# A four-layer graph network on one core: the first tile's table rows fetched in two steps, and the places of the buffers laid out anew

## The chip, the cores and the metric

The kernel runs on one core of a Trainium2 chip. The time is the device time of one execution in microseconds (us), lower is better. The core has five engines with a queue of instructions each: PE (TensorE, matrix products), DVE (VectorE), ACT (ScalarE), POOL (GpSimd) and SP (SyncE, which here only issues transfers). Sixteen DMA engines carry the transfers. POOL issues the gathers, transfers whose rows are picked by a list of indices; SP issues the plain ones.

## The reference

Four graph layers on 2708 nodes with 128 features. Each normalizes x, applies relu to get h, and adds its result to x. `adj` is a 2708 x 2708 matrix. The change lies in the second layer (layer 1):

```python
XW = X @ W
s_col = XW @ a[0, :f]
s_row = XW @ a[0, f:]
Z1 = leaky_relu(s_row[:, None] + s_col[None, :], 0.01)
den = exp(Z1)
num = A @ den
att = where(num != 0, den / where(num != 0, num, 1.0), 0.0)
H = A @ (att @ XW)
```

Layers 0, 2 and 3 are also built on products with `adj`. Layer 2 and layer 3 are one such product each, followed by a 128 x 128 product.

## The kernel before

**Tiles.** A tile is 128 nodes: T = 22 tiles, the last (tile 21) has 20. A stretch of 2708 columns is worked in six blocks of 512 (the last 148), one PSUM bank (`acc0` to `acc5`) each.

**The idea of layer 1.** For a fixed column j, `den[k, j]` depends on k only through whether `s_row[k] + s_col[j]` is positive. So `num[:, j]` needs no product with `den`: if the nodes k are sorted by falling `s_row`, it is a combination of two neighbouring rows of a table of running sums. The kernel ranks the nodes, and `fetch` (L1589) gathers the rows of `adjT` in rank order, 125 per tile, to tiles called `mov`. `make_knots(t)` (L1702) multiplies them by a triangular weight, which gives 128 table rows ("knots", three places of a tile repeat its neighbour's), copies them out of PSUM on DVE and ACT by turns, puts the last two rows into the next `mov` tile, and SP writes them to a table in device memory (L1735). Tile t of the table is rows 128t to 128t + 127; the last one has 96 rows. The last two tiles' writes and the first's are cut in two halves. Each row has 2708 floats, 10.8 KB.

**Which rows a node needs.** ACT counts for every column node how many row scores are above the negative of its own (`signs_of`, L1564 on). `row_places` (L1678 on) turns the count q into the number of the first of the two rows, `pair_u`. Places grow with q. It runs for tiles 0 to 7 behind `make_knots(5)`, for 8 to 15 behind `make_knots(12)`, and for the rest behind `make_knots(18)`. `knots_around` gathers two floats per node and is issued on POOL, at most three per turn of the loop.

**The loop around the seam** (L1740 on) does, for each t: fetch tile t + 3, up to three `knots_around`, `make_knots(t)`, then signs, places, weights. Every instruction that matters is recorded in program order on its engine (`pin`, `Ordered`, L84), so the lines of the code are the order of the queues.

**The last pass of layer 1** (L1775 on) takes the tiles in the order 21, 0, 1, ..., 20 (`ORDER`). `gather(t)` (L1786) fetches the two rows of every node of tile t in one packet per node, 21.7 KB, into a pair buffer of 128 x 2 x 2708 floats; there are three. `divided` (DVE) combines the two rows into an attention tile, `inverted` (ACT) takes a logarithm and an exponential, `limited` (DVE) finishes, `weighed` (PE) multiplies with XW. Attention tiles and, later, the chunks of `adj` come from a pool of five (`big`). Three gathers are issued ahead, the next always behind the `divided` that frees its pair buffer. All gathers read `table[:, :]`, so they wait until the last table row is written.

**The places.** Up to the seam `big` has four buffers. Behind the last table the pools of layer 1 (`l1`), of the rows (`rows`, from which the table is written) and `big` are closed, `big` is opened again with five buffers, and the pair buffers are laid over the rest.

**Behind the pass** the chunks of `adj` for the product A @ (att @ XW) are loaded by SP: three while the pass ends (L1863), then in `aggregate` (L392). Of its 22 chunks the last six (16 to 21) are "resident": they are loaded once into a pool `t_res` (L1879) and stay for layers 2 and 3. Chunks 16 to 18 are asked for behind the fourth chunk.

Of the kernel before, what the change touches and what calls it, by code (L numbers as in the profile page):

```python
# [17 lines left out]
P = 128  # L18
# [6 lines left out]
def kernel(  # L25
# [18 lines left out]
    nc = tc.nc  # L44
    N, D = x.shape
    assert D == P
    T = -(-N // P)
# [5 lines left out]
    TAIL_RES = 6  # L53
# [10 lines left out]

    lay = ctx.enter_context(tc.tile_pool(name="lay", bufs=1))

    big_open = ExitStack()
    big = big_open.enter_context(tc.tile_pool(name="big", bufs=4))
    dram = ctx.enter_context(tc.tile_pool(name="dram", bufs=1, space=DRAM))
    ps_s = ctx.enter_context(tc.tile_pool(name="ps_s", bufs=2, space=PSUM))  # L70
    ps_a = ctx.enter_context(tc.tile_pool(name="ps_a", bufs=1, space=PSUM))
# [14 lines left out]
    pe, dve, act = Ordered(nc.tensor), Ordered(nc.vector), Ordered(nc.scalar)  # L86

    resident = {}
    pools = {}
# [4 lines left out]
    def chunk(i):  # L94
        if i in resident:
            return resident[i]
        if i >= T - pools["n"]:
            c = resident[i] = pools["res"].tile([P, N + 1], F32, name=f"res{i}")
        else:
            c = big.tile([P, N + 1], F32, name="chunk", tag="big")  # L100
        t = tile_at(i)
        pin(nc.sync.dma_start(c[: width(t), :N], adjT[t * P : t * P + width(t), :]))
        if i == T - 1:
            pools["apart"] = True
        return c
# [133 lines left out]
    with nc.allow_non_contiguous_dma(reason="256 elements"):  # L239
# [16 lines left out]
        out=above, in_=ones_b, pattern=[[1, P]], compare_op=ALU.is_ge, fill=0.0, base=-1, channel_multiplier=-1  # L256
# [17 lines left out]
    for v, first, fill in ((1, 3, float(P // 2)), (2, 2, -1e5)):  # L274
        nc.gpsimd.affine_select(
            out=empty[:, v, :], in_=empty[:, v, :], pattern=[[0, T]],
# [3 lines left out]
            out=empty[:, v, :], in_=empty[:, v, :], pattern=[[-PER, T]],  # L280
# [389 lines left out]
    c = len(COLS) - 2  # L670
# [127 lines left out]
    for t in range(T):  # L798
        w = width(t)
# [170 lines left out]
    def vec(name, n=T, dt=F32):  # L970
        return keep.tile([P, n], dt, name=name)
# [718 lines left out]

    def knots_around(t):
        w = width(t)
        pin(
            nc.gpsimd.indirect_dma_start(
                out=around[:w, t, :],
                out_offset=None,
                in_=knot_at[:, :],
                in_offset=bass.IndirectOffsetOnAxis(ap=knot_u[:w, t : t + 1], axis=0),
            )
        )  # L1700

    def make_knots(t):  # L1702
        m = moving.pop(t)
        o = rowtile("knots")
        p = [acc(b) for b in range(NKB)]
        for b, (k0, n) in enumerate(KBS):
            pe.matmul(p[b][:, :n], wt[:, t, :], m[:, k0 : k0 + n], start=True, stop=(t > 0))
        if t == 0:
            pieces = []
            for b, (k0, n) in enumerate(KBS):  # L1710
                inside = []
                for g in range(4):
# [16 lines left out]
        for b, (k0, n) in enumerate(KBS):  # L1729
            (dve.tensor_copy if b % 2 else act.copy)(o[:, k0 : k0 + n], p[b][:, :n])  # L1730
            if t < T - 1:
                dve.tensor_copy(moving[t + 1][:2, k0 : k0 + n], o[:2, k0 : k0 + n])
        n = P if t < T - 1 else LAST
        for c in (slice(0, HALF), slice(HALF, N)) if t in (0, T - 2, T - 1) else (slice(0, N),):
            pin(nc.sync.dma_start(table[t * P : t * P + n, c], o[:n, c]))  # L1735

    BATCHES = {5: (0, 8), 12: (8, 16), 18: (16, T)}
    unsigned = list(range(1, T))
    near = []
    for t in range(T):  # L1740
        if t + 3 < T:
            fetch(t + 3)
        for _ in range(min(len(near), 3)):
            knots_around(near.pop(0))
        make_knots(t)
        for _ in range(2 if t in (3, 7) else 1):
            if unsigned:
                signs_of(unsigned.pop(0))
        if t in BATCHES:
            row_places(*BATCHES[t])  # L1750
            near.extend(range(*BATCHES[t]))
        if t % 4 == 0 and t // 4 + 1 < NG:
            weights(t // 4 + 1)
        if t % 3 == 2 and t // 3 < NG:
            weighted(t // 3)
# [16 lines left out]
    act.activation(row_all, row_all, AF.Exp, bias=forty)  # L1772


    l1.close()  # L1775
    rows_open.close()
    big_open.close()
    big = ctx.enter_context(tc.tile_pool(name="big", bufs=5))
    between = ExitStack()
    pairs = between.enter_context(tc.tile_pool(name="pairs", bufs=3, side="right"))  # L1780
    pools.clear()
    pools.update(n=TAIL_RES)
    py = [acc(b) for b in range(NKB)]
    rows, attention = {}, {}

    def gather(t):  # L1786
        w = width(t)
        r = rows[t] = pairs.tile([P, 2, N], F32, name="pair", tag="pair")
        pin(
            nc.gpsimd.indirect_dma_start(  # L1790
                out=r[:w].rearrange("p a n -> p (a n)"),
                out_offset=None,
                in_=table[:, :],
                in_offset=bass.IndirectOffsetOnAxis(ap=pair_u[:w, t : t + 1], axis=0),
            )
        )
# [8 lines left out]
    def divided(t, some=slice(0, 3)):  # L1805
        w = width(t)
        r = rows[t]
        if t not in attention:
            attention[t] = big.tile([P, N + 1], F32, name="att", tag="big")
        at = attention[t]  # L1810
        for c in cuts(t)[some]:
            dve.scalar_tensor_tensor(
                at[:w, c], r[:w, 0, c], kap[:w, t : t + 1], r[:w, 1, c], op0=ALU.mult, op1=ALU.add
            )
# [29 lines left out]
                stop=(t == ORDER[-1]),  # L1844
            )

    for t in ORDER[:3]:
        gather(t)
    for x_, t in enumerate(ORDER[:-1]):
        divided(t)  # L1850
        if x_ + 3 < T:
            gather(ORDER[x_ + 3])
        inverted(t)
        if x_:
            limited(ORDER[x_ - 1])
            weighed(ORDER[x_ - 1])
    t, u = ORDER[-2:]
    first, rest_ = slice(0, 1), slice(1, 3)
    for i in range(3):
        c = big.tile([P, N + 1], F32, name="chunk", tag="big")  # L1860
        if i == 0:
            dve.memset(c[:1, :1], 0.0)
        pin(nc.sync.dma_start(c[:, :N], adjT[i * P : (i + 1) * P, :]))  # L1863
        resident[i] = c
        if i == 0:
            limited(t, first)
            divided(u, first)
            inverted(u, first)
            limited(t, rest_)
            weighed(t)  # L1870
            divided(u, rest_)
            inverted(u, rest_)
# [3 lines left out]


    tl = ctx.enter_context(ExitStack())
    pools.update(res=tl.enter_context(tc.tile_pool(name="t_res", bufs=1)))  # L1879
    yT = lay.tile([P, N], F32, name="yT", tag="U")  # L1880
    attended = lay.tile([P, T, D], F32, name="attended", tag="Y")
    for b, (k0, n) in enumerate(KBS):
# [135 lines left out]
```

## Time and profile before

| What | us |
|---|---|
| Median of 3 runs (1101.18 to 1101.49) | 1101.22 |
| The profiled execution, its time | 1102.7 |
| Its span in the profile | 1101.0 |
| Last table write issued | 616.2 |
| First pair gather issued on POOL | 621.6 |
| Pair gathers: number, POOL busy | 22, 66.6 |
| DVE waits for pair gathers, total | 21.5 |
| End of the pass on PE (the first product behind it starts) | 778.4 |

The profile shows one execution. Starts are counted from the start of the span. A line of the timeline gives the start, the duration, the engine, the line of the code, the operation, what is written from what, and in brackets how long the engine had been idle and what released it. A line of the stretch view gives the busy time of every engine between two moments, the share of full clock that PE was granted, the mean busy share of the 16 DMA engines, and what they moved in GB/s. Lines of helpers (L84) stand for many operations: there the names of the tiles tell them apart.

### The profile page before, as it was taken

The page shows a single profiled execution, that of the slowest core. Times are in us where ns is not written, and L with a number is a line of the kernel's source. Part 1 is how long each engine was busy: PE and PEld are TensorE (multiplying, and loading weights), DVE is VectorE, ACT ScalarE, POOL GpSimd, SP SyncE. Part 2 cuts the span into 40 slices and gives each one's busy share as a digit, 9 for nine tenths or more (in the row PEclk, how much of TensorE's full clock was granted, in tenths as well). Part 3 has the DMA queues.
Part 4 walks back from the last instruction along what each step waited for, and adds up shares of the span by engine and source line. Part 5 has one row for each costly group of instructions (what it writes and reads, how often), then busy time and mean ns, then how long its engine had stood idle before and what let it go on. Part 6 is the DMA issues. An engine that isn't in the chain of part 4 may idle for free.

```text
span 1101.0 us, 10182 instructions
## 1 busy us (share of the span) xinstructions
PE 998.3 (91%) x3553; PEld 487.2 (44%) x3553; DVE 584.2 (53%) x1203; ACT 403.0 (37%) x637; POOL 230.9 (21%) x248
## 2 busy tenths in 40 slices
PE   6989999999989988899887378778999999999998
PEld 5444444444344454544343133333444455455444
DVE  4366368999852266757466489999310321032003
ACT  6010045444300066568765288788100210021000
POOL 2000000000298781023233245551000000000000
PEclk9999999999999998989999759999999999999999
DMA  9988120005389249389999799998999257716811
GB/s 274 344 319 268 46 82 1 0 1 196 133 353 408 93 148 408 136 336 425 418 415 407 280 430 434 432 428 357 426 368 387 101 209 277 263 60 214 301 42 51
DMA packets 48323, 282.72 MB, mean 257 GB/s; under 512 B 6478, under 2 KB 17834, under 8 KB 28660
## 3 DMA queue, kind: packets, MB, share of 16 engines
q1 hardware_dynamic: 38191, 189.13, 45.7%
q0 software_dynamic: 9840, 92.94, 21.0%
q8 instruction: 28, 0.46, 0.2%
q14 instruction: 24, 0.20, 0.0%
q10 hardware_dynamic: 240, 0.00, 0.0%
HBM read 250.06 MB, written 33.00 MB: 257 GB/s over the span
## 4 chain that ended last, share of the span: by engine, by line
PE 62%; DMA 22%; DVE 9%; issue 3%; ACT 3%; POOL 1%; SPq 0%; DVEq 0%; POOLq 0%; ACTq 0%
PE acc L404 30%; PE acc L84 16%; DMA pair<-table,pair_u 11%; PE acc L806 10%; DMA mov<-in_adj_dram,src_u 5%; DMA chunk<-in_adj_dram 3%; PE ps L84 3%; DVE att L84 3%; PE ps L384 1%; DVE top_i L843 1%; DMA held<-in_adj_dram 1%; PE acc L814 1%; ACT sg L1567 1%; DMA gath<-ydr,near_p 1%; ACT knots L84 1%
## 5 line engine op out<-in xcount | busy, mean ns | idle before, releaser
L84 PE MATMUL acc<-att,xw 128*128 128x512 f32 (+3 forms) x264 | 113.8, 587 | 47.9 <-DVE att L84 47.9
L404 PE MATMUL acc<-chunk,h 128*128 128x512 f32 (+1 forms) x384 | 148.0, 542 | 0.0
L84 PE MATMUL acc<-mov,wt 128*128 128x512 f32 (+1 forms) x264 | 111.6, 569 | 18.8 <-DVE mov L84 17.6
L806 PE MATMUL acc<-zT 128*128 128x512 f32 (+2 forms) x264 | 112.3, 559 | 0.0
L404 PEld LDWEIGHTS acc<-chunk,h 128*128 128x128 f32 x384 | 68.8, 190 | 74.1 <-issue 74.1
L84 PEld LDWEIGHTS acc<-att,xw 128*128 128x128 f32 (+1 forms) x264 | 51.4, 202 | 110.3 <-issue 82.3
L942 POOL DMA_INDIRECT gath<-ydr,near_u x63 | 65.1, 1034 | 153.9 <-DMA ydr<-y 140.6
L404 PE MATMUL acc<-chunk,y 128*128 128x512 f32 x204 | 81.2, 559 | 3.8 <-DMA chunk<-in_adj_dram 2.9
L84 PEld LDWEIGHTS acc<-mov,wt 128*128 128x128 f32 x264 | 48.3, 195 | 81.7 <-DVE mov L84 42.3
L1790 POOL DMA_INDIRECT pair<-table,pair_u x22 | 66.6, 3026 | 76.4 <-DVE att L84 63.6
L821 ACT COPY strip<-acc 128x512 f32<-128x512 f32 (+1 forms) x132 | 60.4, 560 | 59.2 <-issue 35.8
L84 DVE SCALAR_TENSOR_TENSOR att<-pair,kap 128x2708 f32<-128x2708 f32 (+3 forms) x28 | 67.7, 2432 | 21.9 <-DMA pair<-table,pair_u 21.5
L84 DVE COPY mov<-knots 2x512 f32<-2x512 f32 x126 | 47.6, 402 | 52.3 <-DMA mov<-in_adj_dram,src_u 28.3
L404 PE MATMUL acc<-chunk,attended 128*128 128x512 f32 x192 | 73.6, 543 | 0.7 <-DMA chunk<-in_adj_dram 0.7
L84 ACT ACTIVATE att<-att,sca 128x2708 f32<-128x2708 f32 (+3 forms) x28 | 57.8, 2065 | 36.4 <-DVE att L84 36.4
L823 DVE MAX8 top_v<-strip 128x8 f32<-128x2708 f32 (+1 forms) x22 | 64.7, 2965 | 7.3 <-ACT strip L821 7.3
L84 DVE SCALAR_TENSOR_TENSOR att<-row_all,inv_s,att 128x2708 f32<-128x2708 f32 (+3 forms) x28 | 67.6, 2427 | 0.4 <-ACT att L84 0.4
L806 PEld LDWEIGHTS acc<-zT 128*128 128x128 f32 (+1 forms) x264 | 45.1, 185 | 51.3 <-issue 43.8
L84 ACT ACTIVATE att<-att,hb 128x2708 f32<-128x2708 f32 (+3 forms) x28 | 57.9, 2069 | 0.9
L404 PEld LDWEIGHTS acc<-chunk,y 128*128 128x128 f32 x204 | 37.7, 195 | 46.5 <-issue 45.2
L1567 ACT ACTIVATE sg<-row_all,c_nat 128x2708 bf16<-128x2708 f32 (+1 forms) x22 | 56.4, 2564 | 0.1
L84 ACT COPY knots<-acc 128x512 f32<-128x512 f32 x66 | 37.2, 594 | 43.4 <-PE acc L84 41.0
(380 smaller groups left out, 1274.8 us busy)
## 6 DMA issues: line engine op xcount, KB each, us to landing
chunk<-in_adj_dram SPq DMA_DIRECT2D x75, 1354.0 KB
table<-knots SPq DMA_DIRECT2D x19, 1354.0 KB
res<-in_adj_dram SPq DMA_DIRECT2D x9, 1354.0 KB
held<-in_adj_dram SPq DMA_DIRECT2D x11, 512.0 KB
held<-in_adj_dram SPq DMA_DIRECT2D x16, 256.0 KB
upper<-in_adj_dram SPq DMA_DIRECT2D x4, 842.0 KB
held<-in_adj_dram SPq DMA_DIRECT2D x3, 1024.0 KB
chunkY<-in_adj_dram SPq DMA_DIRECT2D x2, 1354.0 KB
```

What stands on the lines that cost most here:

```text
L84: return lambda *a, **k: pin(getattr(self.engine, name)(*a, **k))
L384: mm = nc.tensor.matmul(p[: width(t), t - t0, :], srcT[:, cols(t)], w, start=True, stop=True)
L404: nc.tensor.matmul(out[b][:, :n], y[r, tile_at(i), :], chunk(i)[r, k0 : k0 + n], start=(i == 0), stop=(i == T - 2),)
L806: mm = nc.tensor.matmul(zz[b][:w, :n], zT[:, cols(t)], zT[:, k0 : k0 + n], start=True, stop=False)
L814: nc.tensor.matmul(zz[b][:w, :n], ones_b[g : g + 3, :w], sq_rows[g : g + 3, k0 : k0 + n], start=False, stop=True,)
L821: copied = nc.scalar.copy(s[:w, k0 : k0 + n], zz[b][:w, :n])
L823: nc.vector.max(top_v[:w, t, :], s[:w, :])
L843: pin(nc.vector.max_index(top_i[:w, t, :], top_v[:w, t, :], strips[t][:w, :]))
L942: nc.gpsimd.indirect_dma_start(out=g[: idx.shape[0], :], out_offset=None, in_=ydr[:, :], in_offset=bass.IndirectOffsetOnAxis(ap=idx, axis=0),)
L1567: nc.scalar.activation(sg[:w, :], row_all[:w, :], AF.Sign, bias=c_nat[:w, t : t + 1], accum_out=signs[:w, t : t + 1],)
L1790: nc.gpsimd.indirect_dma_start(out=r[:w].rearrange("p a n -> p (a n)"), out_offset=None, in_=table[:, :], in_offset=bass.IndirectOffsetOnA ...
```

## The change

The change has two parts.

**The first full tile's gather is cut in two.** Tile 0's pairs are fetched by two gathers into the same buffer. The first is put on POOL's queue ahead of `make_knots(20)`, behind that turn's `knots_around`; it reads `table[:2432]` (tables 0 to 18) and leaves out the nodes whose pair lies behind it (a bound on the index). The second stands at the head of the gathers behind the last table and takes the rest by a second list of indices, `pair_b`, in which the nodes already served are moved out of bounds. `rest_of_first`, two DVE operations on one column, makes the list behind the first `row_places`. The order of issue becomes rest of tile 0, tile 21, tile 1.

**The places are laid out anew.** `l1` is closed behind `make_knots(0)`, and a pool `first` with one pair buffer (`lead`) is opened in its place. `big` stays open with four buffers; a pool `extra` has the fifth, and `place` gives every fifth tile from it. `pairs` keeps two buffers and `lead` is the third of the cycle. Later the first two resident chunks (16 and 17) lie in `lead`, and four in `t_res`.

```diff
-    big_open = ExitStack()
-    big = big_open.enter_context(tc.tile_pool(name="big", bufs=4))
+    big = ctx.enter_context(tc.tile_pool(name="big", bufs=4))
...
+    BEGUN = P * (T - 3)
+    pair_b = vec("pair_b", 1, U32)
+    rows = {}
+
+    def rest_of_first():
+        b = vec("rest_of_first", 1)
+        dve.tensor_scalar(b, q[:, 0:1], BEGUN + 0.5, 2.0 * P * T, op0=ALU.is_lt, op1=ALU.mult)
+        dve.scalar_tensor_tensor(pair_b, q[:, 0:1], -1.0, b, op0=ALU.add, op1=ALU.add)
+
+    def gather_first(idx, rows_of_table):
+        pin(
+            nc.gpsimd.indirect_dma_start(
+                out=rows[0].rearrange("p a n -> p (a n)"),
+                out_offset=None,
+                in_=table[:rows_of_table, :],
+                in_offset=bass.IndirectOffsetOnAxis(ap=idx, axis=0),
+                bounds_check=rows_of_table - 1,
+                oob_is_err=False,
+            )
+        )
...
+        if t == T - 2:
+            rows[0] = lead.tile([P, 2 * (N + 1)], F32, name="first", tag="pair")[
+                :, : 2 * N
+            ].rearrange("p (a n) -> p a n", a=2)
+            gather_first(pair_u[:, 0:1], BEGUN)
         make_knots(t)
+        if t == 0:
+            l1.close()
+            lead = ctx.enter_context(tc.tile_pool(name="first", bufs=1))
...
             row_places(*BATCHES[t])
+            if BATCHES[t][0] == 0:
+                rest_of_first()
...
-    l1.close()
     rows_open.close()
-    big_open.close()
-    big = ctx.enter_context(tc.tile_pool(name="big", bufs=5))
+    extra = ctx.enter_context(tc.tile_pool(name="extra", bufs=1))
     between = ExitStack()
-    pairs = between.enter_context(tc.tile_pool(name="pairs", bufs=3, side="right"))
+    pairs = between.enter_context(tc.tile_pool(name="pairs", bufs=2, side="right"))
...
+    def place(name):
+        placed[0] += 1
+        own = placed[0] % 5 == 0
+        return (extra if own else big).tile([P, N + 1], F32, name=name, tag="big")
...
-    def gather(t):
+    def gather(x_):
+        t = ORDER[x_]
+        if t == 0:
+            gather_first(pair_b, P * (T - 1) + LAST)
+            return
         w = width(t)
-        r = rows[t] = pairs.tile([P, 2, N], F32, name="pair", tag="pair")
+        rows[t] = (lead if x_ % 3 == 1 else pairs).tile(
+            [P, 2 * (N + 1)], F32, name="pair", tag="pair"
+        )[:, : 2 * N].rearrange("p (a n) -> p a n", a=2)
...
-    for t in ORDER[:3]:
-        gather(t)
+    for x_ in (1, 0, 2):
+        gather(x_)
     for x_, t in enumerate(ORDER[:-1]):
         divided(t)
         if x_ + 3 < T:
-            gather(ORDER[x_ + 3])
+            gather(x_ + 3)
...
-    pools.update(res=tl.enter_context(tc.tile_pool(name="t_res", bufs=1)))
+    pools.update(res=Residents(tl.enter_context(tc.tile_pool(name="t_res", bufs=1))))
```

`Residents` hands out the two halves of one tile of `lead` for the first two resident chunks, and tiles of `t_res` for the others.

More of the change, by code (lines that the diff above doesn't have):

```diff
@@ L99, in chunk @@
         else:
-            c = big.tile([P, N + 1], F32, name="chunk", tag="big")
+            c = pools["place"]("chunk") if "place" in pools else big.tile(
+                [P, N + 1], F32, name="chunk", tag="big"
+            )
         t = tile_at(i)
@@ L1735, in make_knots @@
             pin(nc.sync.dma_start(table[t * P : t * P + n, c], o[:n, c]))
+    BEGUN = P * (T - 3)
[15 more added lines that the diff above has]
+            )
+        )
     BATCHES = {5: (0, 8), 12: (8, 16), 18: (16, T)}
@@ L1772 @@
     act.activation(row_all, row_all, AF.Exp, bias=forty)
-    l1.close()
     rows_open.close()
-    big_open.close()
-    big = ctx.enter_context(tc.tile_pool(name="big", bufs=5))
+    extra = ctx.enter_context(tc.tile_pool(name="extra", bufs=1))
     between = ExitStack()
-    pairs = between.enter_context(tc.tile_pool(name="pairs", bufs=3, side="right"))
+    pairs = between.enter_context(tc.tile_pool(name="pairs", bufs=2, side="right"))
     pools.clear()
-    pools.update(n=TAIL_RES)
-    py = [acc(b) for b in range(NKB)]
-    rows, attention = {}, {}
-    def gather(t):
+    placed = [0]
+    def place(name):
+        placed[0] += 1
+        own = placed[0] % 5 == 0
+        return (extra if own else big).tile([P, N + 1], F32, name=name, tag="big")
+    pools.update(n=TAIL_RES, place=place)
+    py = [acc(b) for b in range(NKB)]
+    attention = {}
+    def gather(x_):
[3 more added lines that the diff above has]
+            return
         w = width(t)
-        r = rows[t] = pairs.tile([P, 2, N], F32, name="pair", tag="pair")
+        rows[t] = (lead if x_ % 3 == 1 else pairs).tile(
+            [P, 2 * (N + 1)], F32, name="pair", tag="pair"
+        )[:, : 2 * N].rearrange("p (a n) -> p a n", a=2)
         pin(
             nc.gpsimd.indirect_dma_start(
-                out=r[:w].rearrange("p a n -> p (a n)"),
+                out=rows[t][:w].rearrange("p a n -> p (a n)"),
                 out_offset=None,
@@ L1808, in divided @@
         if t not in attention:
-            attention[t] = big.tile([P, N + 1], F32, name="att", tag="big")
+            attention[t] = place("att")
         at = attention[t]
@@ L1859 @@
     for i in range(3):
-        c = big.tile([P, N + 1], F32, name="chunk", tag="big")
+        c = place("chunk")
         if i == 0:
@@ L1878, with __init__, tile @@
     tl = ctx.enter_context(ExitStack())
-    pools.update(res=tl.enter_context(tc.tile_pool(name="t_res", bufs=1)))
+    class Residents:
+        def __init__(self, pool):
+            self.pool, self.two, self.n = pool, None, 0
+        def tile(self, shape, dtype, name):
+            self.n += 1
+            if self.n > 2:
+                return self.pool.tile(shape, dtype, name=name)
+            if self.n == 1:
+                self.two = lead.tile([P, 2 * (N + 1)], F32, name="pair", tag="pair").rearrange(
+                    "p (a n) -> p a n", a=2
+                )
+            return self.two[:, self.n - 1, :]
+    pools.update(res=Residents(tl.enter_context(tc.tile_pool(name="t_res", bufs=1))))
     yT = lay.tile([P, N], F32, name="yT", tag="U")
```

## The prediction

> **What bounds the kernel now.** I read the page first. In the share of busy time PE stands at 91%, but that is a mean over stages. The chain of work that ended last gives PE 62% and DMA 22%, and the costliest DMA item in it is the pair gather.
>
> ```profile
> PE acc L404 30%; PE acc L84 16%; DMA pair<-table,pair_u 11%; PE acc L806 10%; DMA mov<-in_adj_dram,src_u 5%; DMA chunk<-in_adj_dram 3%; PE ps L84 3%; DVE att L84 3%; PE ps L384 1%; DVE top_i L843 1%; DMA held<-in_adj_dram 1%; PE acc L814 1%; ACT sg L1567 1%; DMA gath<-ydr,near_p 1%; ACT knots L84 1%
> ```
>
> So I asked for busy time by stretch around the seam (columns: PE, PEld, DVE, ACT, POOL busy, granted clock, DMA share, GB/s).
>
> ```profile
> 604.00:611.00 7.00, 5.25 (x13) 2.29 (x14) 4.47 (x11) 1.76 (x3) 4.26 (x5) 1.00 0.81 326
> 611.00:616.00 5.00, 4.83 (x12) 1.94 (x12) 4.34 (x11) 1.56 (x3) 0.00 (x0) 1.00 0.89 355
> 616.00:620.50 4.50, 0.00 (x0) 0.00 (x0) 3.31 (x12) 1.30 (x3) 0.00 (x0) 0.80 0.77 251
> 620.50:623.00 2.50, 0.00 (x0) 0.00 (x0) 0.00 (x0) 1.66 (x1) 1.06 (x2) 0.50 0.00 0
> 623.00:628.00 5.00, 0.00 (x0) 0.00 (x0) 0.00 (x0) 0.00 (x0) 1.74 (x2) 0.50 0.95 212
> 628.00:641.00 13.00, 0.05 (x1) 0.08 (x1) 9.00 (x3) 8.17 (x4) 3.80 (x2) 0.50 1.00 428
> 641.00:758.00 117.00, 94.71 (x216) 42.59 (x216) 107.77 (x38) 92.94 (x39) 59.97 (x18) 0.92 1.00 430
> ```
>
> From 628 to 758 the DMA engines never rest (share 1.00, 430 GB/s), while DVE, the next busiest, has 107.8 us of 117. The last pass is a stream of gathers, and its end is the start of the stream plus what each DMA engine must carry. The seam is where the stream starts: nothing moves from 620.5 to 623, and the next 5 us run at half rate. The timeline of POOL gives the issues:
>
> ```profile
> 608.57 0.91 POOL L1694 DMA_INDIRECT around<-knot_at,knot_u  x1 [0.30 <-issue]
> 621.63 0.90 POOL L1790 DMA_INDIRECT pair<-table,pair_u  x1 [12.15 <-DMA table<-knots]
> 622.83 0.96 POOL L1790 DMA_INDIRECT pair<-table,pair_u  x1 [0.30 <-issue]
> 624.10 0.95 POOL L1790 DMA_INDIRECT pair<-table,pair_u  x1 [0.30 <-issue]
> 632.02 0.94 POOL L1790 DMA_INDIRECT pair<-table,pair_u  x1 [6.97 <-DVE att L84]
> 638.14 3.48 POOL L1790 DMA_INDIRECT pair<-table,pair_u  x1 [5.18 <-DVE att L84]
> ```
>
> and that of DVE what follows them:
>
> ```profile
> 628.72 3.03 DVE L84 SCALAR_TENSOR_TENSOR att<-pair,kap 20x2708 f32<-20x2708 f32 x1 [9.21 <-DMA pair<-table,pair_u]
> 634.83 3.04 DVE L84 SCALAR_TENSOR_TENSOR att<-pair,kap 128x2708 f32<-128x2708 f32 x1 [3.08 <-DMA pair<-table,pair_u]
> 637.78 3.02 DVE L84 SCALAR_TENSOR_TENSOR att<-row_all,inv_s,att 20x2708 f32<-20x2708 f32 x1
> 641.30 3.04 DVE L84 SCALAR_TENSOR_TENSOR att<-pair,kap 128x2708 f32<-128x2708 f32 x1 [0.50 <-DMA pair<-table,pair_u]
> ```
>
> POOL waits for the last table write, then issues tile 21 (20 rows), tile 0 and tile 1. DVE divides them at 628.7, 634.8 and 641.3, and from there a tile takes 6.45 us. The trace's records of single DMA packets say why: each pair row is one packet of 21,664 bytes taking 0.805 us, and in the records eight of them run back to back on each of 16 engines per tile: 8 x 0.805 = 6.44.
>
> **The first step holds few rows.** If all of tile 0 were in before the last table landed, the stream would start 6.44 us earlier. How many rows are in the tables below row 2432 (tables 0 to 18) is a matter of data, so I worked it out with the reference's formulas from its inputs. With c the column scores and r the row scores of layer 1, q is the number of r above -c, and the first row of a pair is q + 3 x round((q + 63)/125) - 1. Column scores average +0.25, row scores 0.00, both with a spread of 0.13: most q are large. Of tile 0's 128 nodes 23 fall into tables 0 to 18, 17 into table 19, 22 into 20 and 66 into 21. The first step fetches **23 rows**, and **105 remain** for after the last table.
>
> **Whom the 23 rows help.** Rows that a bounded gather leaves out keep their places in the engines' queues. The last fetch of moving rows shows it: its empty places pass as 4-byte packets of 7 to 9 ns, one between each two table packets, and the full rows are not spread out anew. So engine by engine tile 0 has still 8 rows, and what counts after the table is the engine with most late rows. With engines taking 8 neighbouring rows each, the late ones are 5 4 6 7 8 8 7 4 7 6 8 7 8 7 7 6; with every sixteenth row, 6 7 7 8 6 8 7 7 6 7 7 5 7 6 5 6. Both have engines with 8. A gather has landed when its slowest engine has, so the stream behind tile 0 starts no earlier: **gain 0**. The 20 rows of tile 21 ran as two packets on each of ten engines; if those miss the engines with 8, the longest load falls from 10 packets to 9, 0.8 us. Were the rows spread evenly, 23/16 x 0.805 = 1.2 us. I take 0 and keep 1.2 as the other end.
>
> [...]
>
> **What the first step costs.** POOL is free for it at 609.8, behind six gathers of knots (the last ends at 609.48); table 18's packets are done by 606.7, so it doesn't wait. Nothing but the other pair gathers is behind it on POOL. From issue to first packet took 1.6 us (621.63 to 623.23), so its packets run from 611.4, among the writes of tables 19 to 21 on the same engines; reads and writes alternate packet by packet in the records of 600 to 605. By the layouts above an engine gets up to 3 or 4 of the 23 rows: 4 x 0.805 = 3.2 us. Idle on a mean engine from 611.4 to 620.5 is 0.11 x 4.6 + 0.23 x 4.5 = 1.5 us, and about 0.4 of that lies behind its last write. So the last write, at 620.1 now, comes 3.2 - 1.5 + 0.4 = 2.1 us later at most; if the write packets of 616 to 619, at 0.3 us and more where 0.23 was usual, make up some of it, 0.6. I take **1.3 us**. Lower end 0 (writes served first), upper end as in the second rival. This delay carries over whole, since every later gather waits for the table.
>
> **What is late next.** After the table, the order is rest of 0, tile 21, tile 1: three issues before, three now. Tile 21 now stands behind up to 8 rows and lands when tile 0 did, 634.8 instead of 628.7 (all plus the delay). DVE divides 21 at 634.8 and 0 at 637.8; ACT then needs 5.1 us for 21, so limiting 21 runs at 643.1 and tile 1, which landed at 641.3, is divided at 646.1, 4.8 us late. The fourth gather issues at 638.1 instead of 632.0, with first packets at 639.8; tile 1's last packets ran to about 640.9, so the engines that set the pace find work in time, by 1.1 us. DVE's two passes can follow each other in 2 x 2.96 us against 6.45, so it wins back 0.5 us a tile and is level after some ten of 20. PE begins 5 us later, at the 0.5 clock that the stretch view shows, and has 4.8 us a tile at full clock to catch up. Cost 0; without the 1.1 us, as much as is lacking.
>
> **The rest.** Two DVE operations on 128x1 behind the first row_places: nearest row 0.17 us, 0.35 in all, hidden since the next table waits 21.6 us for its fetch (530.55 in the chain); bare, 0.35. Place keeps the order of five attention buffers (four and one), and the pair buffers keep a cycle of three. The first two resident chunks use the pair buffer of tile 18, free long before; SP issues them behind the fourth chunk (772.43) as before: 0. Two loads into one tile might wait for each other; the three issues took 1.33 us in all, one landing more would be about 3 us, against a PE that waited 0.7 us for chunks in this pass: -0 to +2, I take 0.
>
> **Sum.** 0 gained, 1.3 lost: profiled execution 1102.7 (span 1101.0) to 1104.0, and on the median 1101.2 **to 1102.5**. Own range 1100.6 (even spread, 0.6 delay) to 1103.3 (2.1).
>
> **Rivals.**
> 1. *Faster: the first step pays the slow start.* Packets at 623.2 to 627.5 took 1.2 to 2.2 us, not 0.805, about four an engine: 4 x 0.8 = 3.2 us. If that belongs to the first reading of the table and not to engines coming out of idleness, it is paid beside the writes: -3.2 + 0.6 = 1098.6. Against it: the first chunk packets after the idle of 764 took up to 1.6 us for 0.41, with no table involved. Chance 0.12. It decides if packets after the table are at 0.8 us at once.
> 2. *Slower: reads among writes are slow too.* At 1.6 us a packet, as at 623, 4 rows take 6.4, less 1.1: +5.3 at most, middle of this and the main case +3.3, 1104.5. For it: write packets stretch in 616 to 619. Against: reads at 600 to 605 kept their 0.41. Chance 0.25.
> 3. *Slower: table writes 20 and 21 wait for the gather.* If the reading of part of the table holds back writes to other parts, the first step lands at about 618 and 3 MB of writes follow: +6, 1107.2. Against: rows are named in the access. Chance 0.07.
> 4. *The step does nothing*: 23 rows displace nothing, 1101.2. Chance 0.10.
> The forecast has 0.46.
>
> A run of this kernel can be told from no change at about 0.2%, 2.2 us. Faster is rival 1: 0.12. Slower is rivals 2 and 3 and an eighth of the forecast's: 0.38. The rest, 0.50, is within. The range leaves out rivals 1 and 3 (0.19): 1100.0 to 1106.5, its top rival 2's +5.3.
>
> **What would show it.** Right: a gather at about 610 on POOL; the last table write 0.6 to 2.1 us later against the last fetch; DVE's first pair division 6 us later against it; tile 1 divided near 646 + 1.3, then spacing under 6.45 until level; stream of gathers ending about 1.3 us later. Wrong: tile 21 divided within 8 us of the last table write (few late rows); POOL's first step waiting past 612; SP's table issues held up; DMA share below 1.00 between 640 and 650 (a fourth gather too late), which would add its gap.

## The result and the profile after

| | before | after |
|---|---|---|
| Median of 6 runs each, us | 1102.4 (1101.18 to 1108.53) | 1121.43 (1118.03 to 1126.32) |
| Ratio, 95% interval | 1 | 1.0161 [1.0125, 1.0196] |
| Profiled execution: time, span | 1102.7, 1101.0 | 1122.07, 1120.3 |
| Last table write: its last packet ends | 620.11 | 623.71 |
| First gather issued behind the table | 621.63 | 624.96 |
| First division on DVE | 628.72 | 640.81 |
| Last packet of the pair gathers ends | 764.35 | 783.39 |
| From that first issue to that last packet ("the pass") | 142.72 | 158.43 |

The changed kernel is slower by 1.6%, and the time lies outside the range forecast. In all tables, medians and ratios leave out single runs at a lower granted clock that took over 1.5% longer than the fastest of the same kernel. Of 19.3 us of span, 3.3 are there when the first gather is issued, 15.7 more come in the pass, and behind it 0.3. The stretch view of after (columns as before: PE, PEld, DVE, ACT, POOL busy, granted clock, DMA share, GB/s):

```profile
624.00:626.50 2.50, 0.00 (x0) 0.00 (x0) 0.00 (x0) 0.00 (x0) 1.24 (x2) 0.50 0.00 0
626.50:640.00 13.50, 0.00 (x0) 0.00 (x0) 0.00 (x0) 0.00 (x0) 1.66 (x2) 0.50 1.01 297
640.00:650.00 10.00, 0.00 (x0) 0.00 (x0) 6.94 (x3) 6.10 (x3) 4.43 (x2) 0.50 0.53 197
650.00:660.00 10.00, 7.88 (x10) 3.16 (x11) 10.00 (x4) 8.92 (x4) 4.72 (x1) 0.50 1.01 433
660.00:670.00 10.00, 10.00 (x22) 4.66 (x21) 9.76 (x4) 8.41 (x5) 10.00 (x1) 0.77 0.17 71
670.00:680.00 10.00, 6.85 (x19) 3.11 (x17) 0.00 (x0) 1.98 (x1) 2.45 (x3) 1.00 0.90 342
...
690.00:770.00 80.00, 61.25 (x152) 27.89 (x151) 73.81 (x25) 63.21 (x25) 43.84 (x13) 0.99 1.01 429
```

Read down the DMA column. Before, the stream had share 1.00 from 628 on. Now it falls to 0.53 between 640 and 650 and to 0.17 between 660 and 670, and in that last stretch DVE is busy for 9.76 us of 10 and POOL for all 10, with a single instruction. The timeline of POOL names it:

```profile
613.00 1.04 POOL L1749 DMA_INDIRECT first<-table,pair_u  x1 [1.85 <-issue]
624.96 1.00 POOL L1749 DMA_INDIRECT first<-table,pair_b  x1 [10.91 <-DMA table<-knots]
626.26 0.90 POOL L1833 DMA_INDIRECT pair<-table,pair_u  x1 [0.30 <-issue]
627.47 0.99 POOL L1833 DMA_INDIRECT pair<-table,pair_u  x1 [0.30 <-issue]
644.10 3.50 POOL L1833 DMA_INDIRECT pair<-table,pair_u  x1 [15.64 <-DVE att L83]
647.90 0.94 POOL L1833 DMA_INDIRECT pair<-table,pair_u  x1 [0.30 <-issue]
655.28 15.30 POOL L1833 DMA_INDIRECT pair<-table,pair_u  x1 [6.44 <-DVE att L83]
670.88 0.94 POOL L1833 DMA_INDIRECT pair<-table,pair_u  x1 [0.30 <-issue]
672.12 0.94 POOL L1833 DMA_INDIRECT pair<-table,pair_u  x1 [0.31 <-issue]
```

The second column is how long an issue lasts: 0.9 to 1.0 us at the seam, 3.50 and then **15.30** in the pass. The longest in the pass of before was 3.49. The two issues behind it started only at 670.88 and 672.12, so two more pair buffers that came free meanwhile stayed empty until then. In the records of single packets no pair packet moves from 662.75 to 671.28, 8.53 us, and none from 646.38 to 648.30, 1.92 us. Before, there was no such hole between the first packet and the last. The timeline of DVE beside it:

```profile
640.81 3.03 DVE L83 SCALAR_TENSOR_TENSOR att<-pair,kap 20x2708 f32<-20x2708 f32 x1 [20.70 <-DMA pair<-table,pair_u]
643.76 3.02 DVE L83 SCALAR_TENSOR_TENSOR att<-first,kap 128x2708 f32<-128x2708 f32 x1
649.03 3.03 DVE L83 SCALAR_TENSOR_TENSOR att<-row_all,inv_s,att 20x2708 f32<-20x2708 f32 x1 [2.25 <-ACT att L83]
651.99 3.02 DVE L83 SCALAR_TENSOR_TENSOR att<-pair,kap 128x2708 f32<-128x2708 f32 x1
654.94 3.02 DVE L83 SCALAR_TENSOR_TENSOR att<-row_all,inv_s,att 128x2708 f32<-128x2708 f32 x1
...
666.74 3.02 DVE L83 SCALAR_TENSOR_TENSOR att<-row_all,inv_s,att 128x2708 f32<-128x2708 f32 x1
680.12 3.04 DVE L83 SCALAR_TENSOR_TENSOR att<-pair,kap 128x2708 f32<-128x2708 f32 x1 [10.36 <-DMA pair<-table,pair_u]
```

From 649.03 to 669.76 DVE runs without idle time, no line behind that of 649.03 has a bracket: seven operations, each starting 0.07 us before the one ahead of it ends (654.94 against 651.99 + 3.02 = 655.01). The issue of 655.28 ends at 670.58, which is 0.82 us behind the end of the last of them. So POOL's issue did not finish while DVE ran without a pause, and DVE paused only when the data that this issue should have fetched were missing. Then DVE stands idle for 10.36 us. The chain of waits shows the price (start, length, what):

```profile
655.28 24.72 DMA pair<-table,pair_u
680.00 0.03 issue
...
683.43 16.53 DMA pair<-table,pair_u
```

The chain goes by every third gather, from its issue to its landing. Such a piece takes about 16 us when nothing is in the way (16.53 here, 15.9 to 16.0 in before); the one with the long issue takes 24.72.

Two holes, 1.92 + 8.53 = 10.45 us, make up two thirds of the 15.7. Counted on a mean DMA engine by the records of single packets, the 15.7 are three terms. Idle time in the pass is 16.3 us against 3.5 in before, 12.8 more, and the holes are most of it. What pair packets of the pass take above 0.805 us each adds up to 6.7 us against 2.7, 4.1 more; over half of the 6.7 lies at 632 to 640, where the median packet took 1.51 us. And the 23 packets that the first step had already fetched are 1.2 us less.

### The profile page after: what moved, and what is told of

Its sections match the earlier page's. It is cut to its first block, busy times and chain, and to the rows that moved or that the text cites. A ratio compares the mean times of both kernels' runs of the same rounds, so it can differ in the third digit from the quotient of the medians.

```text
span 1120.3 us, 10204 instructions
## 1 busy us (share of the span) xinstructions
PE 996.9 (89%) x3553; PEld 486.6 (43%) x3553; DVE 582.9 (52%) x1205; ACT 402.5 (36%) x637; POOL 239.7 (21%) x249
## 5 line engine op out<-in xcount | busy, mean ns | idle before, releaser
L1833 POOL DMA_INDIRECT pair<-table,pair_u x21 | 72.4, 3447 | 73.1 <-DVE att L83 71.6
L83 DVE SCALAR_TENSOR_TENSOR att<-pair,kap 128x2708 f32<-128x2708 f32 (+3 forms) x27 | 64.6, 2408 | 38.3 <-DMA pair<-table,pair_u 38.3
```

The source lines that it names most:

```text
L83: return lambda *a, **k: pin(getattr(self.engine, name)(*a, **k))
L1833: nc.gpsimd.indirect_dma_start(out=rows[t][:w].rearrange("p a n -> p (a n)"), out_offset=None, in_=table[:, :], in_offset=bass.IndirectOff ...
```

## The experiments

**Theory.** The order of the first gathers makes DVE start late; a late DVE runs without pauses; POOL's issues then wait for it, and the stream of gathers stops. **Rivals.** (a) The first step among the table writes costs the time. (b) The new places do. (c) DVE's late start costs it directly, without POOL. In the tables below the ratio is to the kernel before on the same chip; "no packet" is the longest hole in the pair stream within the pass.

### The order, the two steps and the places, one at a time

The order alone, on the kernel before:

```diff
-    for t in ORDER[:3]:
+    for t in (ORDER[1], ORDER[0], ORDER[2]):
```

> The kernel before with one edit: the three gathers ahead are issued in the order tile 0, tile 21, tile 1; no first step, the places as before. Theory L (late DVE, starved issue): in the changed kernel tile 21 stands behind tile 0's rows, DVE begins some 6 us late and then runs without a pause, and while it does so POOL cannot finish issuing a gather (15.3 us for one issue at 655), so the DMA engines run dry. By L this kernel shows it too: first division 6 us later than before, one POOL issue of over 8 us, a stretch of several us without DMA traffic, time 1107 to 1117. Rival F (first step: the cut gather and its 23 packets among the table writes cost the time): 1101 to 1103. Rival P (the new places cost it): 1101 to 1103.

The changed kernel with the small tile first (the two steps and the places stay):

```diff
-    for x_ in (1, 0, 2):
+    for x_ in (0, 1, 2):
```

> The changed kernel with one edit: behind the last table the order is tile 21, rest of tile 0, tile 1. L: tile 21 lands some 7 us after its issue, DVE has no lag, all issues on POOL stay at 0.9 to 3.5 us, time 1102 to 1106 (what is left is the delay of the table writes by the first step). F and P: 1116 to 1122, as the changed kernel.

The same without the two steps, so the new places alone:

```diff
-            gather_first(pair_u[:, 0:1], BEGUN)
...
-                rest_of_first()
...
-        if t == 0:
-            gather_first(pair_b, P * (T - 1) + LAST)
-            return
```

> The changed kernel's places and buffers, but tile 0 is fetched in one gather behind the last table, in the order of before (21, 0, 1). P: 1110 or more. L and F: 1101 to 1103, the places cost nothing.

| | median, us | ratio | longest issue, us | no packet, us | pass, us | write: issue to last packet, us |
|---|---|---|---|---|---|---|
| before | | 1 | 3.49 | 0 | 142.72 | 3.87 |
| after | 1121.43 | 1.0161 [1.0125, 1.0196] | 15.30 | 8.53 | 158.43 | 6.87 |
| e1, order alone | 1118.47 | 1.0121 [1.0075, 1.0167] | 15.30 | 8.25 | 158.14 | 4.36 |
| e2, two steps and places | 1102.71 | 0.9987 [0.9944, 1.003] | 3.50 | 0 | 141.14 | 7.05 |
| e3, places alone | 1100.76 | 0.9964 [0.9919, 1.0008] | 3.50 | 0 | 142.25 | 3.50 |

The timeline of POOL in e1, without a first step and with the old places:

```profile
640.35 3.50 POOL L1790 DMA_INDIRECT pair<-table,pair_u  x1 [15.24 <-DVE att L84]
651.57 15.30 POOL L1790 DMA_INDIRECT pair<-table,pair_u  x1 [6.49 <-DVE att L84]
```

The same two issues, to the hundredth. The order alone reproduces the loss (1118.47, a little more than the 1107 to 1117 expected), and with the old order it is gone: rivals (a) and (b) fall. The last column gives what the first step does cost: the last write takes about 7 us with it, 3.5 to 4.4 without, some 3 us more. The profiles of all kernels here agree: 6.87 to 7.42 us in the eleven with that step, 3.50 to 4.67 in the nine without it or with a later one (e6). The gain shows in the pass: 1.1 us shorter in e2 than in e3, 1.6 than in before. That covers about half of the cost; the intervals of e2 and e3 overlap, so no net cost of the two steps is shown.

### Is it POOL's issue, or DVE's lateness by itself?

In e4 `limited` leaves out the second half of the columns for the first seven tiles, so that DVE has less to do there and can't run without pauses:

```diff
-        for c in cuts(t)[some]:
+        for c in [slice(0, N // 2)] if t in ORDER[:7] else cuts(t)[some]:
```

> The changed kernel; for the first seven tiles of the order (21, 0 to 5) the limiting leaves out the second half of the columns, so that DVE has pauses while it catches up. L: no issue on POOL of over 6 us behind the first lagging tiles, the stretch without DMA traffic at 662 to 671 is gone, time 7 to 12 us under the changed kernel: 1109 to 1115. F and P: 1118 to 1123.

1113.32 us, 1.008 [1.0034, 1.0126]. The issue in the place of the 15.30 took 0.94, and the next of its kind:

```profile
663.83 2.08 POOL L1833 DMA_INDIRECT pair<-table,pair_u  x1 [5.62 <-DVE att L83]
```

2.08 for 3.49: shorter by 1.41, as DVE's operation is shorter by 1.40 (1.62 for 3.02). Both lasted as long as the rest of DVE's operation and 0.81 to 0.82 us. The long hole is gone, the pass takes 149.2. That is 9 us less than in after. What is left, 6.5 over before, is 3.1 of slow packets (5.8 us on a mean engine) and 4.5 of idle time, a hole of 1.96 in it, less the 1.2 of the 23 packets. But a DVE with less to do also catches up sooner, so e4 alone doesn't settle rival (c).

In the next run DVE keeps its work, and one element is copied behind each division, which waits for the division's result:

```diff
+        dve.tensor_copy(at[:1, N : N + 1], at[:1, N - 1 : N] if some != slice(0, 1) else at[:1, 0:1])
```

> The changed kernel with one tiny DVE copy (one element, which reads what the division just wrote) behind every division, so that DVE's row of operations has a short gap per tile; no work is left out. The measured rows of the idle operations at the seam say that an issue on POOL gets in at any gap between two DVE operations, and waits only as long as each begins before its predecessor ends. L in that form: no issue on POOL over 4 us, the empty stretch of 8.5 us is gone, time 1108 to 1114, 7 to 12 us under the changed kernel's 1121. If DVE's load or the DMA queue holds the issue: 1118 to 1124, since DVE has more work than before.

The longest issue was 3.67, the long hole was gone, the pass took 148.87; but the time, 1118.78, 1.0121 [1.0083, 1.0159], was far from the 7 to 12 us expected. So it was taken again beside the changed kernel, with two controls.

> The changed kernel itself, as the control for the three below on the same chip. Both theories: the ratio seen before, 1.013 to 1.020, with one issue of 15.30 us on POOL.

> The changed kernel with a one-element DVE copy behind every division, so that DVE's operations do not begin before their predecessor ends. Theory (the 8.5 us without a packet are paid whole at the end): 6 to 10 us below the changed kernel on the same chip, about 1.008 of the kernel before. Rival (given back later, by a DVE that lags behind the stream): within 3 us of the changed kernel.

> The small tile gathered first again, and the same copies: what the copies themselves cost where no issue is held. Theory: 0 to 3 us over the kernel before (22 copies, each with the wait for what it reads). If the copies cost 5 us or more here, the rival of the run above is wrong, and the copies' own price hides the gain there.

> The kernel before with nothing changed but the order of the first gathers (0, 21, 1), and the same copies. Theory: no issue over 4 us on POOL, no 8 us without a packet, 5 to 9 us below the order alone (1.012 of before), so about 1.005. Rival: 1.012 as without the copies.

| | median, us | ratio | longest issue | pass, us |
|---|---|---|---|---|
| c1, the changed kernel | 1122.18 | 1.0144 [1.0094, 1.0193] | 15.30 | 158.98 |
| c2, with the copies | 1118.58 | 1.0096 [1.0059, 1.0134] | 3.67 | 148.81 |
| c3, copies, small tile first | 1111.01 | 1.0042 [1.0015, 1.0068] | 3.67 | 141.30 |
| c4, before, order alone, copies | 1110.45 | 1.0039 [1.0016, 1.0062] | 3.67 | 148.28 |

The copies shorten the pass by 10 us in both pairs (c1 to c2, e1 to c4), while DVE starts as late (its first division comes 15.2 to 16.3 us behind the first issue in all four) and does more. So rival (c) falls for these 10 us, and so does a full DMA queue as what holds the issue, since the copies change nothing there. The other 5.6 to 6 us by which the passes of c4 and c2 are longer than before's are not shown to come from POOL's issue.

In the time, c4 lies 0.8% below e1, about 9 us as expected; the intervals are apart, though the two ran on different chips. c2 lies 3.6 us below c1 by the medians and 0.48% by the ratios, less than the 6 expected, and the intervals overlap. The reason is a price of the copies, and c3 shows it: it has no held issue to lose, was expected 0 to 3 us over before, and stands at 1.0042, 0.55% above e2 without copies (from different chips, intervals that just overlap). In the profiles it lies behind the pass. From the last pair packet to the end of the span c2 and c3 take 342.1 and 342.4 us, e5 340.9, against 336.5 in c1 and 337.1 in e2, and 336.8 in c4, which has the copies at the old places. PE waits there 3.7 and 4.3 us for chunks of `adj` in c2 and c3, 0.6 in c1, 0.4 in c4. Why the chunks are late with the copies and the new places together stays open. So the long issue costs 9 to 10 us by the pass, and about 9 by the time where nothing else hides it (e1 to c4); in c1 to c2 the copies give 5.6 of it back.

### What on DVE holds the issue?

Four kernels, of one run each, put idle work on an engine just behind the last table, on the kernel before, where its three first issues come; the result goes to a spare tile. One edit is shown, the others differ in its last line and the count.

```diff
     rows, attention = {}, {}
+    spot = big.tile([P, N + 1], F32, name="spot", tag="big")
+    wide = wt.rearrange("p t f -> p (t f)")[:, :N]
+    for _ in range(5):
+        dve.scalar_tensor_tensor(spot[:, :N], wide, 0.5, wide, op0=ALU.mult, op1=ALU.add)
```

> The kernel before, with five idle DVE operations (scalar_tensor_tensor, 128x2708 floats, two tensor inputs in SBUF, result never read) put on DVE behind the last operation of the table stage, about 619.5 to 634.5, beside the first three gather issues on POOL. No computation is left out. L: the first gather issue on POOL lasts until DVE's row of operations ends, 12 us or more in place of 0.9. Rival (the issue waits for DMA or for a place in the queue, not for DVE): 0.9 us as before.

> The same with nine tensor_scalar operations, 128x2708 floats, one tensor input, 1.6 us each (twice the rate per element of the former). If the issue is held by any DVE operation that works two elements at a time or with two inputs: held, 12 us or more. If only two inputs hold it: 0.9 us.

> [...] If any busy DVE holds the issue: 12 us or more. [...]

> The control: six activations of 128x2708 on ACT in the same place, none on DVE. L: POOL issues at 0.9 us each, the first division at the usual distance from the last table write (12 us behind its issue); the inversion of tile 21 on ACT waits.

| idle work | time, us (before: 1100.68) | first three issues, us | longest issue later |
|---|---|---|---|
| m1, DVE, two-input operation, 3.0 us x5 | 1112.83 | 1.75, 2.78, 2.69 | 15.30 |
| m2, DVE, `tensor_scalar`, 1.6 us x9 | 1105.64 | 2.71, 2.93, 2.91 | 3.50 |
| m3, DVE, `max` (128x2708 in, 128x8 out), 3.0 us x5 | 1115.77 | 0.90, 0.97, 0.95 | 15.30 |
| m4, ACT, six activations | 1115.71 | 0.90, 0.97, 0.95 | 15.30 |

The timeline of POOL in m1, then in m3:

```profile
618.97 1.75 POOL L1794 DMA_INDIRECT pair<-table,pair_u  x1 [12.09 <-DMA table<-knots]
621.02 2.78 POOL L1794 DMA_INDIRECT pair<-table,pair_u  x1 [0.30 <-issue]
...
646.44 15.30 POOL L1794 DMA_INDIRECT pair<-table,pair_u  x1 [6.49 <-DVE att L84]
```

```profile
621.41 0.90 POOL L1794 DMA_INDIRECT pair<-table,pair_u  x1 [12.79 <-ACT row_all L84]
...
647.97 15.30 POOL L1794 DMA_INDIRECT pair<-table,pair_u  x1 [6.48 <-DVE att L84]
```

Three things follow. In these runs a busy DVE held an issue only in some operations: in m3 it was as busy as in m1 (five of 3.0 us), and the issues took 0.90 to 0.97 us. In m1 I expected 12 us or more and was wrong: the issue of 618.97 ended 0.77 us behind the end of one idle operation (619.95), though the next began at once. These idle operations all write the same tile, and each starts 0.034 us after the one before ends; those of the pass start 0.07 before. And the same long issue of 15.30 appears in m1, m3 and m4, kernels without any part of the change: what they share is that DVE gets late against the stream. In m4 nothing was put on DVE; ACT's inverting is late instead. Lateness isn't enough, though: in m2 DVE's first division came as late behind the first issue as in m3 (12.15 and 12.06 us), and no issue lasted over 3.50. There one division (650.83) began at the very end of its predecessor, not 0.07 us before it, and the issue got in there. The timelines of POOL and DVE in m2:

```profile
648.15 3.49 POOL L1794 DMA_INDIRECT pair<-table,pair_u  x1 [6.49 <-DVE att L84]
```

```profile
647.81 3.02 DVE L84 SCALAR_TENSOR_TENSOR att<-row_all,inv_s,att 128x2708 f32<-128x2708 f32 x1
650.83 3.04 DVE L84 SCALAR_TENSOR_TENSOR att<-pair,kap 128x2708 f32<-128x2708 f32 x1
```

m2's `tensor_scalar` took 1.6 us for as many elements as took the two-input operation of m1 3.0, and it held the issues: each ended 0.10 to 0.12 us behind the second end of an operation that it met. The `max` of m3, with one input like m2's operation and as long as m1's, held none. Beside two-input operations, in m1 and in the steady 3.49, an issue ended 0.77 to 0.84 us behind the end of one, nearly as long as a free issue lasts in all (0.90 to 1.05). Which property of an operation makes it hold an issue, and what part of the issue waits, no run shows; nor does one show why in after it was held over five operations on end.

### What lets the issue in?

With the copies the gap isn't where the issue got in. The timelines of POOL and DVE in c2:

```profile
657.16 3.67 POOL L1833 DMA_INDIRECT pair<-table,pair_u  x1 [6.44 <-DVE att L83]
```

```profile
656.93 0.14 DVE L83 COPY att<-att 1x1 f32<-1x1 f32 x1
657.00 3.02 DVE L83 SCALAR_TENSOR_TENSOR att<-row_all,inv_s,att 128x2708 f32<-128x2708 f32 x1
659.95 3.02 DVE L83 SCALAR_TENSOR_TENSOR att<-pair,kap 128x2708 f32<-128x2708 f32 x1
```

The issue ends at 660.83, 0.81 behind the operation of 657.00, although the next began at 659.95, 0.07 before that one ended. It had begun 0.16 us into the operation, 0.34 in after. So the moment was moved, with a POOL operation ahead of each later gather of the pass (here 128x8; 128x512 in d2; d3 without the copies):

```diff
+        if x_ > 2:
+            pin(nc.gpsimd.memset(rows[t][:, 0, :8], 0.0))
```

> c2 with a short POOL operation (128x8, written only) ahead of every gather of the pass, so that the issue begins later in DVE's operation than the 0.16 us of c2. If what lets an issue in is that it begins early in an operation (0.16 us in c2, 0.34 us in the changed kernel, where it was held): issues now last to the end of the next operation but one, 5 to 6.5 us. If it is the copy itself, wherever the issue begins: 2.5 to 3.5 us, as in c2 less the shift.

> The same with a longer POOL operation (128x512), so that the issue begins still later, about the middle of the operation. By the moment of the issue: about 4.5 to 5.5 us. By the copy: 1.5 to 3 us.

> The changed kernel with the short POOL operation and no copies: the control. Both: one issue held until DVE has run out of data, some 14 to 15 us, and a time near that of the changed kernel (1.013 to 1.02 of the kernel before).

The issue that answers to the long one took 3.19 in d1, 0.65 us into its operation, 3.09 in d2, 0.75 into it, and without the copies, in d3:

```profile
654.52 14.81 POOL L1835 DMA_INDIRECT pair<-table,pair_u  x1 [0.60 <-POOL pair L1833]
```

In the range tried (0.16 to 0.75 us into the operation with the copies, 0.34 and 0.83 without) the moment of the issue doesn't decide, the copies do: 3.19 and 3.09 fit the second expectation of d1 (2.5 to 3.5), and 3.09 is just above that of d2, since d2's shift came out smaller than meant. How one copy behind every second operation makes an opening at a boundary where none shows is not settled. Times: d1 1114.61, 1.0098 [1.0069, 1.0128]; d2 1118.62, 1.0126 [0.9989, 1.0262]; d3 1119.03, 1.0129 [0.9998, 1.0261]; the last two intervals are too wide to tell anything apart.

### Can the first step be made to pay?

With the small tile first, the first step was put one turn of the loop later, where it takes more rows (62 early, 66 late, worked out as in the prediction):

```diff
-    BEGUN = P * (T - 3)
+    BEGUN = P * (T - 1)
...
-        if t == T - 2:
+        if t == T - 1:
```

> Order 21, rest of 0, tile 1, and the first step put one table later and with a bound of 2688 in place of 2432, so that it waits for table 20 and its packets run behind most of the last writes, in the 3 us in which no packet moves: 62 rows early, 66 late, at most 6 of one engine's 8 by the layouts considered. Expected: last table write 0 to 1.5 us later, the stretch from the first issue behind the table to the last pair packet 2 to 3 us shorter than with one gather (142.3 and 142.7 us), time 0.998 of the kernel before (0.996 to 1.001). If a first step always costs what it gains: 1.000 or more.

```profile
616.49 1.24 POOL L1749 DMA_INDIRECT first<-table,pair_u  x1 [9.17 <-DMA table<-knots]
619.28 0.91 POOL L1833 DMA_INDIRECT pair<-table,pair_u  x1 [1.56 <-DMA table<-knots]
624.62 1.05 POOL L1749 DMA_INDIRECT first<-table,pair_b  x1 [4.43 <-DMA pair<-table,pair_u]
```

1105.45 us, 0.9991 [0.9968, 1.0015]: no gain shown. The last write took 3.98 us, as without a first step, but the pass took 142.38, not 2 to 3 us less than with one gather (142.3 and 142.7), as expected. On this timeline of POOL the rest of tile 0 is issued only at 624.62, 4.43 us after POOL was free, and what released it is the landing of a pair gather, which can only be the small tile's or the first step. Last, e2 with the first step issued twice, to price it:

```diff
+            gather_first(pair_u[:, 0:1], BEGUN)
```

> Order 21, rest of 0, tile 1, with the first step issued twice (the same 23 rows twice into the same buffer). The last table write took 7.5 us from issue to landing with one first step and 4.2 to 4.5 without. If the first step's packets among the writes cause the delay: 9 to 11 us with two, time 2 to 4 us over the kernel with one. If it is chance: 4 to 8 us as before.

1110.61 us, 1.0058 [1.003, 1.0085]. The second copy waited 6.97 us for the first to land and was issued at 619.47; its packets began at 621.2, when the last write, which ended at 622.19, was all but done. So that write took 7.12 us, as with one step, not the 9 to 11 expected. The rest of tile 0 then waited 4.50 us, and the pass, from 623.51 on, took 143.95. The run does not price a second step among the writes.

## Why the prediction was wrong

- **The step that failed** is in "What is late next": "DVE's two passes can follow each other in 2 x 2.96 us against 6.45, so it wins back 0.5 us a tile and is level after some ten of 20", and with it "Cost 0; without the 1.1 us, as much as is lacking". The first half is what happened: DVE ran gapless from 649.03. But POOL's issue did not end until this run of operations ended, so the DVE that caught up stopped the stream it was to catch up with. It had been in the lines I showed: the issue of 638.14 lasted 3.48 where those at the seam took 0.90 to 0.96, and I used only its start. 638.14 + 3.48 = 641.62 is 0.82 behind the end of the operation that DVE had begun at 637.78, as every later one is. Measured: 10.45 us of holes, the order alone +1.21% [0.75, 1.67].
- The same part has "in time, by 1.1 us": the fourth gather was forecast to issue at 638.1 in before's time, with packets at 639.8. With the 3.3 us by which the first gather was late that is 641.4. It issued at 644.10, 2.7 later, since tile 21 came in late behind the slow packets (divided at 640.81, not 638.1), and it took 3.50 beside the division of tile 0. Its first packets came at 648.3, and the engines had been empty for 1.92 us.
- **The first step's rows** were right: 23 packets of 21,664 bytes went in the first step.
- **Its cost**, 1.3 us with bounds 0 and +5.3, was mis-sized: these packets took 1.57 us on the mean (0.81 to 3.14), not 0.805, and the last write came some 3 us later against its issue (6.87 and 7.05 in after and e2, 3.50 to 4.36 in e3, before and e1). That is near the main case of rival 2, +3.3, and within the bounds; the last packet of the table in after ended 3.6 us later in all, and 0.6 of that was there when the last write was issued (616.84 for 616.24).
- **The gain**, taken as 0 with 1.2 as the other end, measured 1.1 (e2 to e3) to 1.6 (e2 to before): the pass got shorter as if the rows had been spread evenly, so the argument that the fullest engine decides is not borne out by these profiles, one of each kernel.
- **Rival 1**, the slow start paid early, fell: packets behind the table are slow all the same, and with the small tile second more so (in the pass 6.7 us on a mean engine; 2.5 in e2, 2.7 in before). **Rival 3** fell: the last write was issued 0.6 us later, not some 6. The wait of POOL's first step past 612 (it was issued at 613.00, 1.85 us after POOL was free) came; no run shows what it moved.
- **The rest at 0** held: the places alone cost nothing (0.9964 [0.9919, 1.0008]), and behind the pass after loses 0.3 us against before.
- The last sign I named, a DMA share below 1.00 between 640 and 650, did appear, 0.53. I named it, but gave it no rival and no price beyond "its gap".

**What stays open.** Why pair packets at 632 to 640 take 1.51 us at the median when the small tile is gathered second, and where the rest of the longer pass comes from when the long issue is gone; which property of DVE's sequence keeps the issue out over several operations; why the copies cost 4 to 6 us behind the pass with the new places and nothing with the old; and whether the two steps cost or gain a few tenths of a per cent.

## What to carry to other kernels

When an instruction's duration in the trace differs between places (0.94 and 3.49 for the same gather), find what it waits for before the order is changed: here the duration is a wait that the view of idle time doesn't list. An engine that is late and catches up is not free if another engine that feeds it needs its pauses (here 15.30 us for an issue beside a DVE without pauses); "it has slack and wins it back" has to be tested against everything that shares something with it. A small item at the head of a pipeline (here 20 rows of 21,664 bytes against 128) started all engines behind it early: DVE's first division came 7.09 us behind the first issue in before and 15.42 in e1, and putting it second cost 1.2% by itself.

## What the runs showed of the hardware

- A gather's issue on POOL took 0.90 to 1.05 us beside an idle DVE (before, after, e6), 0.90 to 0.97 beside `max` on DVE (m3) and beside ACT's activations (m4); where a two-input operation was under way when it began, it ended 0.77 to 0.84 us after the end of one of them (m1, before, after, e4). Beside gapless ones it ended 15.30 us after it began, to the hundredth, in five kernels (after, e1, m1, m3, m4), in each of which DVE had five operations to do when the issue began, the one under way among them.
- A gap of 0.034 us between operations (m1) let an issue in; a start 0.07 us ahead of the predecessor's end (after) did not, except where one-element copies stood in the sequence (e5, c2, c4, d1, d2).
- Row packets of 21,664 bytes read among table writes took 1.57 us on the mean (after), against 0.805 in the undisturbed stream, and with them the last of those writes took 6.87 us from issue to last packet in after and 7.05 in e2, against 3.50 to 4.36 in e3, before and e1.
